# A fused attention layer on one core: the order of GpSimd's work in the last three units, and the first loads cut in halves over two queues

## The chip, the cores and the metric

The kernel runs on one core of a Trainium2 chip. The metric is the time of one execution on the device in microseconds (us), and the time before is the median of three runs. Beside it stands one profiled execution, whose trace gives the start and length of every instruction.

The engines are named as the profile names them: PE (TensorE; PEld is its weight load), DVE (VectorE), ACT (ScalarE), POOL (GpSimd) and SP (SyncE). SP, ACT and POOL also issue DMAs; SPq and ACTq are the issuing side of the first two. SBUF is the on-chip memory, PSUM the accumulators that PE writes.

## The reference, cut to what matters

```python
# x (8, 512, 512); tokens = cond_1024[:, None, :] (8, 1, 512); 16 heads of 32
Q = split_heads(x @ Wq.T + bq);  tQ = split_heads(tokens @ Wq.T + bq)
K = split_heads(x @ Wk.T + bk);  tK = split_heads(tokens @ Wk.T + bk)
V = split_heads(x @ Wv.T + bv)
scores = einsum('bhqd,bhkd->bhqk', Q + tQ, K + tK) / sqrt(32)
out = einsum('bhqk,bhkd->bhqd', softmax(scores), V)
return x + merge_heads(out)
```

All of it is fp32. The projection of the single token (with twice the bias) is a vector per batch and head that is added to Q and K.

## The kernel before, in words

**Units.** A unit t is one batch and one group of four heads, so there are T = 32 units (8 batches by 4 groups). For a unit the kernel computes the scores twice: first with queries on the partitions (`row_scores`, L641), only to take each row's maximum on DVE (L589, L650, L1289) and, for half of the queries, to take the exponentials as well; then with keys on the partitions (L757, L786, L1272), where PE adds the negated row maxima into the same PSUM bank ahead of the scores, so that ACT only has to take exponentials (L767, L796, L1287).

**The split.** To add the maxima on PE exactly enough, a unit's fp32 maxima (128 partitions by 16 numbers) are cut into three bf16 parts: `split_max` (L710 to L719), four small instructions one behind the other, L716 (cast), L717 (subtract), L718 (cast), L719 (subtract). They run on POOL for most units and on DVE for the last two. The parts are then turned so that queries lie along the free dimension: by a DMA transpose (`turn_max`, L728) for most units, by four PE transposes and a copy (`transpose_max`, L738 and L744) for units 0, 30 and 31. The exponentials of a unit can start only behind that.

**Weighted sums.** The exponentials times V (L801, L817), the row sums, the reciprocal (L1049 and others), a 32x32-block transpose on DVE (L889), a multiplication by the reciprocal and the addition of the residual on POOL (`send`, L890 and L891), and four DMAs to the output (L894). The residual is x plus the bias of V: four DMAs (`load_residual`, L191) and one addition on POOL (`bias_residual`, L204), made ahead of `send`.

**Kept exponentials.** For units 1 to 29 (`KEPT`) half of the exponentials of the first pass are kept. They are turned in 32x32 blocks by DVE (L660) and then six pairs of blocks across the diagonal are exchanged by DMA (`swap_kept`, L683) in three moves of six DMAs each: a block aside, its partner into its place, the block from aside to the partner's. Each move waits for the one before. Some of the eighteen are issued by POOL (software queue), the others by SP.

**Order.** The instructions of PE, ACT, DVE and POOL stand in the order in which the program writes them (`manual_schedule`); each engine runs its list strictly in order. SP's list, DMAs alone, is placed by the scheduler. The DMAs of SP and ACT share eight completion counters in turn, so the ninth DMA issued waits until the first has landed, and so on; at the start of the kernel this holds up an issuing queue.

**The start.** Wq's first block of 128 rows is loaded by SP, x's first block by ACT, then x's second by SP and Wk's first by ACT. Then SP loads the three small vectors (`cond`, `bq`, `bk`, L252 to L254), and the rest follows. PE fills the time until data is there with 28 small bf16 matmuls (L933). Then it transposes Wq's block (L313), two blocks of x (L358), Wk's block (L313) and the small vectors (L950), and goes on with projections (L404). ACT loads its function table between its DMAs and its first copy. Wk's remaining columns and Wv follow on SP in strips of 32 rows, 16 DMAs each (L270). `condition` (L911, L913) projects the token by Wq, and later by Wk.

**The end.** Units 29, 30 and 31 have code of their own (from L1294). In unit 30 PE runs three `crossed` rows (`crossed`, L1255 to L1290), each of which computes unit 30's exponentials for a block of keys while DVE takes unit 31's maxima for a block of queries. Behind the third, `split_max(31)` runs on DVE (L1359 of the program writes it), `transpose_max(31)` on PE, and the last unit's four `exponentials` follow, with sums of exponentials on DVE (`sum_of`, L1244 and L1246) and one of them on POOL. In this part POOL also runs: the bias of three residuals, `send` of units 28, 29 and 30, and the sum just named. Unit 31 is finished apart (L1411 to L1438).

Of the kernel before, what the change touches and what calls it, by code (L numbers as in the profile page):

```python
# [17 lines left out]
def kernel(  # L18
# [39 lines left out]
    P = 128  # L58
# [123 lines left out]
    def load_residual(t):  # L182

        b, g = divmod(t, G)
        if turned_by_vector(t):
            if t >= T - 3:
                xr[t] = late[0][:, (t - T + 3) * 4, :].rearrange("p (f e) -> p f e", e=BL)
            else:
                xr[t] = op.tile([P, NB, BL], F32, tag="xr", name=f"xr_{t}")
            for h in range(HG):  # L190
                nc.sync.dma_start(  # L191
                    xr[t][h * BL : (h + 1) * BL], spread(x[b], g * P + h * BL)
                )
        else:

            xr[t] = xT[b][:, g, :]
# [56 lines left out]
    nc.sync.dma_start(cond_sb[B : B + 1, :], bq.rearrange("(o d) -> o d", o=1))  # L253
    nc.sync.dma_start(cond_sb[B + 1 : B + 2, :], bk.rearrange("(o d) -> o d", o=1))  # L254
    load_x(2)
    load_x(3, nc.scalar)
# [6 lines left out]
    nc.scalar.activation(table, ones[:, :1], AF.Exp)  # L263
    load_w("q", Wq, nc.sync, [2, 3])

    for n, w, f in (("k", Wk, HG), ("v", Wv, 0)):
        wn = ws[n].rearrange("p c (f e) -> p c f e", e=BL)
        for cc in range(NC):
            for h in range(HG):
                nc.sync.dma_start(  # L270
                    wn[h * BL : (h + 1) * BL, cc, f:], spread(w, cc * P + h * BL)[:, f:]
                )
    bvl = const.tile([P, 1], F32, tag="bvl", name="bvl")
# [391 lines left out]
    def swap_kept(t, move, last=nc.gpsimd):  # L665
# [6 lines left out]
        for n, (a, g) in enumerate(APART):  # L672
# [10 lines left out]
            (last if here else nc.sync).dma_start(to, of)  # L683
# [248 lines left out]
    for _ in range(28):  # L932
# [27 lines left out]
    transpose_x(3, bank(3), nc.scalar.copy)  # L960
    first_part("k", pk, 0)
# [168 lines left out]
    def thirds(t, made):  # L1130
# [16 lines left out]
        for i in (1, 2):  # L1147
# [29 lines left out]
            if i == 2:  # L1177
                if r == 0:
                    combine_x(b + 1, 1, nc.gpsimd)
                if t + 1 < KEPT[-1]:  # L1180
                    load_residual(t + 1)
# [53 lines left out]

    for t in KEPT[:-1]:
# [57 lines left out]
    late.append(store[:, 4:8].rearrange("p c i s -> p (c i) s"))  # L1294
# [17 lines left out]
    aparts[t] = masked(t)  # L1312
    swap_kept(t, 2)
    halves_of(t - 1, banks(0), (1,))
# [19 lines left out]
    load_residual(t)  # L1334
# [7 lines left out]
    for u in (t, t + 1):  # L1342
        load_residual(u)
    for u in (t + 1, t - 1):
        bias_residual(u)
# [3 lines left out]
    den = denominators_of(t - 1, banks(1))  # L1349
    row(1)  # L1350
# [4 lines left out]
    send_sums(t - 1, whole[t - 1], den)  # L1355
    bias_residual(t)
# [35 lines left out]
    nc.gpsimd.tensor_tensor(y30, y30, rec.broadcast_to([P, NB, BL]), ALU.mult)  # L1392
# [7 lines left out]
    store_30(nc.sync, (0, 1, 3))  # L1400
# [12 lines left out]
    nc.vector.tensor_tensor(part_x[:, two[1]], pd[:, two[1]], xr[t][:, two[1]], ALU.mult)  # L1413
    store_30(nc.scalar, (2,))
    oT = late[0][:, 2, :]
# [56 lines left out]
```

## Time and profile before

| what | value |
|---|---|
| median of 3 runs | 659.02 us (658.79 to 660.39) |
| the profiled execution's own time | 658.57 us |
| its span, first to last instruction | 656.8 us |
| PE busy | 646.9 us (98%) |
| DVE busy | 600.8 us (91%) |
| ACT busy | 534.6 us (81%) |
| POOL busy | 431.1 us (66%) |
| mean granted PE clock | 0.997 |

The span lies 1.77 us below the execution's own time; that part is around the kernel's instructions. A row of the timeline gives the start in us from the start of the span, the length in us, the engine and line, the operation, output and inputs, shapes, the count of instructions that the row merges, and in square brackets how long the engine sat idle before it and what ended that. Neighbouring rows of one engine can overlap by some hundredths, since an instruction's record runs to its last write.

### The profile page before, as it was taken

To read this page: it belongs to the slowest core of one execution; us is meant where nothing else is said; L and a number is where in the kernel's file an instruction comes from. 1 tells how busy PE (TensorE), PEld (TensorE's weight loads), DVE (VectorE), ACT (ScalarE), POOL (GpSimd) and SP (SyncE) were. 2 spreads that over 40 slices of the span, in tenths; PEclk is the share of its full clock that TensorE was granted. 3 is DMA by queue.
4 is the path that set the end of the run, shared out by engine and by line. 5 is a ranking of instruction groups with operands and counts; after the bars stand their busy time and mean duration, and the time that the engine had idled before them with its cause. 6 is when DMAs were issued, how large, how long until landed. Compare 5 with 4: busy or idle time off the path is not lost.

```text
span 656.8 us, 24923 instructions
## 1 busy us (share of the span) xinstructions
PE 646.9 (98%) x9856; PEld 349.5 (53%) x9856; DVE 600.8 (91%) x832; ACT 534.6 (81%) x1364; POOL 431.1 (66%) x680
## 2 busy tenths in 40 slices
PE   9999999999999999999999999999999999999977
PEld 7355455555555555555555555555555555555522
DVE  4799999999999999999999999999999989899897
ACT  2579888889888888988888898888898888887544
POOL 3633665796766777678757667677676776674651
PEclk9999999999999999999999999999999999999989
DMA  7633698988876787877898777787888767687521
GB/s 189 107 49 59 136 182 159 170 175 180 184 158 158 151 186 172 187 156 165 173 194 166 166 164 171 167 180 150 190 190 182 176 146 163 157 148 185 142 46 33
DMA packets 248458, 102.02 MB, mean 155 GB/s; under 512 B 229963, under 2 KB 230475, under 8 KB 248341
## 3 DMA queue, kind: packets, MB, share of 16 engines
q1 hardware_dynamic: 234724, 65.60, 52.6%
q0 software_dynamic: 12384, 33.83, 19.1%
q8 instruction: 78, 1.28, 0.9%
q10 hardware_dynamic: 1232, 0.98, 0.5%
q14 instruction: 40, 0.32, 0.2%
HBM read 19.75 MB, written 8.39 MB: 43 GB/s over the span
## 4 chain that ended last, share of the span: by engine, by line
PE 97%; DVE 1%; DMA 1%; issue 0%; ACT 0%; SPq 0%; DVEq 0%
PE psum L461 44%; PE psum L641 19%; PE psum L817 16%; PE psum L786 8%; PE psum L775 3%; PE psum L404 2%; PE psum L801 2%; PE psum L757 1%; DMA store<-in_x_dram 1%; PE psum L827 0%; PE psum L754 0%; DVE split L718 0%; PE psum L911 0%; PE psum L1272 0%; PE psum L313 0%; PE psum L852 0%
## 5 line engine op out<-in xcount | busy, mean ns | idle before, releaser
L702 ACT ACTIVATE store<-psum,nmax 128x512 f32<-128x512 f32 x204 | 140.1, 701 | 36.0 <-DVE nmax L589 26.3
L702 ACT ACTIVATE psum<-psum,nmax 128x512 f32<-128x512 f32 x248 | 164.7, 669 | 3.6 <-DVE nmax L589 3.0
L683 POOL DMA_DIRECT2D store<-store x258 | 128.7, 502 | 58.4 <-DMA store<-store 40.7
L589 DVE TENSOR_REDUCE nmax<-psum 128x1 f32<-128x512 f32 x225 | 144.4, 678 | 19.0 <-PE psum L641 16.8
L650 DVE TENSOR_REDUCE nmax<-psum 128x2 f32<-128x1024 f32 x125 | 151.4, 1211 | 0.0
L641 PE MATMUL psum<-kT,qT 32*128 32x512 f32 x1024 | 142.5, 617 | 0.0
L796 ACT ACTIVATE store<-psum 128x512 f32<-128x512 f32 x232 | 119.8, 602 | 26.7 <-PE psum L786 26.7
L660 DVE STREAM_TRANSPOSE store<-store 128x1024 f32<-128x1024 f32 x116 | 138.8, 1216 | 0.0
L817 PE MATMUL psum<-store,v 128*32 128x256 f32 x1856 | 106.8, 381 | 0.0
L817 PEld LDWEIGHTS psum<-store,v 128*32 128x32 f32 x1856 | 57.0, 110 | 57.1 <-ACT wT_q L628 21.2
L890 POOL TENSOR_TENSOR res<-res,recs 128x512 f32<-128x512 f32 x30 | 31.4, 1046 | 66.8 <-DVE res L889 66.7
L641 PEld LDWEIGHTS psum<-kT,qT 32*128 32x128 f32 x1024 | 55.7, 183 | 35.5 <-issue 20.0
L786 PE MATMUL psum<-qT,kT 32*128 32x256 f32 x928 | 59.9, 373 | 0.0
L702 ACT ACTIVATION_READ_ACCUMULATOR psum<-psum,nmax 128x1 f32 x248 | 52.7, 213 | 0.0
L461 PE MATMUL psum<-wc_v,xc 128*32 128x256 f32 x768 | 47.7, 379 | 0.0
L786 PEld LDWEIGHTS psum<-qT,kT 32*128 32x128 f32 x928 | 45.5, 184 | 3.9 <-issue 0.3
L204 POOL TENSOR_TENSOR xr<-xr,bvs 128x512 f32<-128x512 f32 x29 | 37.1, 1280 | 11.4 <-DMA x<-in_x_dram 11.4
L461 PE MATMUL psum<-xc,wc_k 128*32 128x256 f32 x720 | 44.5, 379 | 0.0
L461 PE MATMUL psum<-xc,wc_q 128*32 128x256 f32 x720 | 44.5, 379 | 0.0
L702 ACT ACTIVATION_READ_ACCUMULATOR store<-psum,nmax 128x1 f32 x204 | 43.9, 215 | 0.0
L891 POOL TENSOR_TENSOR res<-res,xr 128x512 f32<-128x512 f32 x29 | 37.1, 1278 | 2.3
L461 PE MATMUL psum<-xT,wT_k 128*32 128x256 f32 x480 | 34.5, 382 | 0.0
(196 smaller groups left out, 1001.4 us busy)
## 6 DMA issues: line engine op xcount, KB each, us to landing
store<-store SPq DMA_DIRECT2D x264, 128.0 KB, 2.6
store<-store POOLq DMA_DIRECT2D x258, 128.0 KB, 3.5
out_dram<-res SPq DMA_DIRECT2D x123, 64.0 KB, 3.6
xr<-in_x_dram SPq DMA_DIRECT2D x116, 64.0 KB, 3.0
x<-in_x_dram SPq DMA_DIRECT2D x112, 64.0 KB, 3.4
w_q<-in_L_cond_Wq_dram SPq DMA_DIRECT2D x4, 256.0 KB, 3.9
w_v<-in_L_cond_Wv_dram SPq DMA_DIRECT2D x16, 64.0 KB, 2.4
w_k<-in_L_cond_Wk_dram SPq DMA_DIRECT2D x16, 48.0 KB, 2.6
```

The lines of the kernel that those rows point to most:

```text
L204: nc.gpsimd.tensor_tensor(xr[t], xr[t], bias, ALU.add)
L461: nc.tensor.matmul(pt[r], still[:, r], moving, start=(kc == kcs[0]), stop=(kc == kcs[-1]))
L589: nc.vector.tensor_reduce(nmax[t][:, qc, j : j + 1, 0], pt, AX.X, ALU.max, negate=True)
L641: nc.tensor.matmul(pt, qkT["q", t][r, qc * P : (qc + 1) * P], qkT["k", t][r, :], start=True, stop=True,)
L650: nc.vector.tensor_reduce(nmax[t][:, qc, pr * 2 : pr * 2 + 2, 0], pt, AX.X, ALU.max, negate=True)
L660: nc.vector.transpose(e, e)
L683: (last if here else nc.sync).dma_start(to, of)
L702: nc.scalar.activation(to, of, AF.Exp, bias=nmax[t][:, qc, j, :], accum_out=sums[t][:, qc, j, :],)
L786: nc.tensor.matmul(bank[j][:, i * HS : (i + 1) * HS], qkT["k", t][r, kc * P : (kc + 1) * P], qkT["q", t][r, rest], start=False, stop=(i == 1),
L796: nc.scalar.activation(e[:, i, :], bank[pr * 2 + i], AF.Exp)
L817: nc.tensor.matmul(pt[j * HD : (j + 1) * HD, half * HS : (half + 1) * HS], vs[b % 2][:, kc, (g * HG + j) * HD : (g * HG + j + 1) * HD], e, ...
L891: nc.gpsimd.tensor_tensor(y, y, xr.pop(t), ALU.add)
```

## The change

At the start: Wq's first block and x's first block each come as two halves of 256 columns, the left halves from SP and the right ones from ACT. x's second, third and fourth block and Wk's first are all issued by SP. The small vectors go from SP to ACT, behind the table load. PE's filling matmuls are 24 and not 28. Six of the sixteen strips of Wk are issued by ACT, behind its copy of x's fourth block. `condition("k")` stands right behind `condition("q")`.

At the end: the bias of the residuals of units 29, 30 and 31 and the load of unit 30's stand in unit 29, ahead of the first `crossed` row, and unit 29's residual is loaded in unit 28; both residuals have other places in SBUF (unit 31's is read from the transposed x and needs no load). `send` of unit 29 stands ahead of the second `crossed` row. Unit 30's multiplication by the reciprocal is on DVE, not on POOL. Two of unit 30's four output DMAs go out from ACT and two from SP (before: one and three). The first half of unit 31's last addition stands ahead of the second half of its residual product. In `swap_kept`, unit 28's last move goes wholly to POOL, three DMAs ahead of `split_max(29)` and three behind; unit 29's first move goes wholly to SP.

```diff
-            if t >= T - 3:
-                xr[t] = late[0][:, (t - T + 3) * 4, :].rearrange("p (f e) -> p f e", e=BL)
+            if t == T - 2:
+                xr[t] = late[0][:, 2, :].rearrange("p (f e) -> p f e", e=BL)
...
-    load_w("q", Wq, nc.sync, [0])
-    load_x(0, nc.scalar)
+    xs[0] = early[:, 3, :]
+    for to, of in ((ws["q"][:, 0, :], Wq[:P, :]), (xs[0], x[0, :P, :])):
+        nc.sync.dma_start(to[:, :HS], of[:, :HS])
+        nc.scalar.dma_start(to[:, HS:], of[:, HS:])
     load_x(1)
     wk0 = early[:, 7, :]
-    nc.scalar.dma_start(wk0, Wk[:P, :])
-
-    cond_sb = early[: B + 2, 0, :]
-    nc.sync.dma_start(cond_sb[:B, :], cond)
...
+    nc.sync.dma_start(wk0, Wk[:P, :])
     load_x(2)
-    load_x(3, nc.scalar)
+    load_x(3)
...
     nc.scalar.activation(table, ones[:, :1], AF.Exp)
+    cond_sb = early[: B + 2, 0, :]
+    nc.scalar.dma_start(cond_sb[:B, :], cond)
+    nc.scalar.dma_start(cond_sb[B : B + 1, :], bq.rearrange("(o d) -> o d", o=1))
+    nc.scalar.dma_start(cond_sb[B + 1 : B + 2, :], bk.rearrange("(o d) -> o d", o=1))
...
+    load_spread("k", Wk, HG, (0, 1))
+    load_spread("k", Wk, HG, (2,), nc.sync, (0, 1))
+    load_spread("v", Wv, 0, range(NC))
...
-            if t < KEPT[-2]:
+            if t < KEPT[-1]:
                 here = move == 2 or move == 0 and n >= later
-            elif t < KEPT[-1]:
-                here = move == 2 and n < 3 or move == 0 and n >= later
             else:
-                here = n >= 3
-            (last if here else nc.sync).dma_start(to, of)
+                here = move > 0 and n >= 3
+            (nc.gpsimd if here else nc.sync).dma_start(to, of)
...
-    for _ in range(28):
+    for _ in range(24):
...
     transpose_x(3, bank(3), nc.scalar.copy)
+    load_spread("k", Wk, HG, (2,), nc.scalar, (2, 3))
+    load_spread("k", Wk, HG, (3,), nc.scalar)
...
     condition("q", bank(6))
+    condition("k", bank(5))
     project_qk_part(1, "q", 0, bank(7))
     condition_end("q", bank(1), nc.vector)
     project_qk_end(0, "q", pq)
-    condition("k", bank(5))
...
-                swap_kept(t, 2)
+                first = range(6 if t + 1 < KEPT[-1] else 3)
+                swap_kept(t, 2, first)
                 split_max(t + 1)
                 turn_max(t + 1)
+                swap_kept(t, 2, range(len(first), 6))
...
     swap_kept(t, 1)
     apart = masked(t - 1)
     aparts[t] = masked(t)
+    load_residual(t + 2)
+    bias_residual(t + 2)
     swap_kept(t, 2)
+    bias_residual(t)
+    load_residual(t + 1)
...
     send_sums(t - 1, whole[t - 1], den)
-    load_residual(t)
+    bias_residual(t + 1)
...
     apart = masked(t - 1)
-    for u in (t, t + 1):
-        load_residual(u)
-    for u in (t + 1, t - 1):
-        bias_residual(u)
     halves_of(t - 1, banks(2), (0,))
     nc.scalar.copy(whole[t - 1][:, :HS], banks(2)[:, :HS])
     spread_sums(apart, banks(1))
     den = denominators_of(t - 1, banks(1))
+    send_sums(t - 1, whole[t - 1], den)
     row(1)
     crossed(t, 1, 2)
     acc = room_for_sums(t)
     sum_of(t, acc, 1, nc.gpsimd, [1])
     part_of(t, banks(2), [0])
-    send_sums(t - 1, whole[t - 1], den)
-    bias_residual(t)
     row(2)
...
-    nc.gpsimd.tensor_tensor(y30, y30, rec.broadcast_to([P, NB, BL]), ALU.mult)
+    nc.vector.tensor_tensor(y30, y30, rec.broadcast_to([P, NB, BL]), ALU.mult)
     nc.gpsimd.tensor_tensor(y30, y30, x30, ALU.add)
...
-    store_30(nc.sync, (0, 1, 3))
+    store_30(nc.sync, (0, 1))
...
-    nc.vector.tensor_tensor(part_x[:, two[1]], pd[:, two[1]], xr[t][:, two[1]], ALU.mult)
-    store_30(nc.scalar, (2,))
+    store_30(nc.scalar, (2, 3))
...
         nc.vector.tensor_tensor(oT[:, two[i]], pv[:, two[i]], part_x[:, two[i]], ALU.add)
+        if i == 0:
+            nc.vector.tensor_tensor(part_x[:, two[1]], pd[:, two[1]], xr[t][:, two[1]], ALU.mult)
```

In the first block of the last part, t is unit 29; from "apart = masked(t - 1)" with the two removed loops on, t is unit 30.

More of the change, by code (lines that the diff above doesn't have):

```diff
@@ L663, with swap_kept @@
     between = store[:, 16:18]
-    def swap_kept(t, move, last=nc.gpsimd):
+    def swap_kept(t, move, some=range(6)):
         later = 6 if t % 4 == 1 else 2
@@ L670, in part @@
             return kept[t][a * BL : (a + 1) * BL, g].rearrange("p c h s -> p (c h s)")
-        for n, (a, g) in enumerate(APART):
+        for n in some:
+            a, g = APART[n]
             at = (n + 2) % HG * BL
@@ L1234, in one_item @@
             other_products(n, b, u, dens, nothing, at, True)
+    late.append(store[:, 4:8].rearrange("p c i s -> p (c i) s"))
     for t in KEPT[:-1]:
@@ L1292, in crossed @@
         row_max_of(u, qc, 1, banks(HG + 2, 2))
-    late.append(store[:, 4:8].rearrange("p c i s -> p (c i) s"))
     t = T - 3
@@ L1412 @@
     nc.scalar.copy(den, pd)
-    nc.vector.tensor_tensor(part_x[:, two[1]], pd[:, two[1]], xr[t][:, two[1]], ALU.mult)
-    store_30(nc.scalar, (2,))
-    oT = late[0][:, 2, :]
+    store_30(nc.scalar, (2, 3))
+    oT = late_part(4)
     y = late[0][:, 1, :].rearrange("p (c s) -> p c s", c=NS)
```

13 lines of the change are left out of this document (5 added, 8 removed).

## The prediction

> **What bounds the kernel now.** I read the page first, then PE's waits, then the timeline of the last 50 us and of the first 10.
>
> ```profile
> PE 97%; DVE 1%; DMA 1%; issue 0%; ACT 0%; SPq 0%; DVEq 0%
> ```
>
> This is the chain of work that ended last, by engine: PE carries 97% of it. So an edit pays only where PE waits or behind PE's last work. The waits of PE's matmuls (who waited for whom, us in total, times, longest) name one place:
>
> ```profile
> PE psum L738 <- DVE split L719: 4.0, 1, 4.0
> ...
> PE psum L313 <- DMA w_q<-in_L_cond_Wq_dram: 0.4, 1, 0.4
> ```
>
> Once, for 4.0 us, PE waits for the split of unit 31's maxima; the short waits are at the start. Between, the reader sees PE saturated, by the stretches of the windows view (stretch, its length, then busy time of PE, PEld, DVE, ACT, POOL, granted clock):
>
> ```profile
> 7.00:30.00 23.00, 23.00 (x133) 13.43 (x136) 13.02 (x25) 6.63 (x15) 13.09 (x12) 1.00 0.68 118
> 600.00:630.00 30.00, 30.00 (x408) 14.94 (x404) 25.85 (x39) 18.39 (x40) 11.85 (x20) 1.00 0.63 139
> ```
>
> From 7 us to 30 us and from 600 us to 630 us PE is busy without a gap. Whatever the change moves there costs or gains nothing, unless it creates a wait.
>
> **The split, -3.73 us.** The split of unit 30 (first and last of its four rows), and then unit 31's, beside what POOL does at that time:
>
> ```profile
> 617.16 0.20 DVE L716 CAST split<-nmax 128x16 bf16<-128x16 f32 x1
> 617.92 0.23 DVE L719 TENSOR_TENSOR split<-rest,split 128x16 bf16<-128x16 f32 x1
> ...
> 630.32 0.20 DVE L716 CAST split<-nmax 128x16 bf16<-128x16 f32 x1
> 630.39 1.26 POOL L204 TENSOR_TENSOR store<-store,bvs 128x512 f32<-128x512 f32 x1 [5.74 <-DMA store<-in_x_dram]
> 630.56 1.13 DVE L717 TENSOR_TENSOR rest<-nmax,split 128x16 f32<-128x16 f32 x1
> ...
> 631.62 2.34 POOL L1244 TENSOR_TENSOR acc<-store 128x1024 f32<-128x1024 f32 x1
> 631.73 2.29 DVE L718 CAST split<-rest 128x16 bf16<-128x16 f32 x1
> 633.92 1.04 POOL L890 TENSOR_TENSOR res<-res,recs 128x512 f32<-128x512 f32 x1
> 634.05 0.99 DVE L719 TENSOR_TENSOR split<-rest,split 128x16 bf16<-128x16 f32 x1
> ...
> 635.10 0.40 PE L738 MATMUL psum<-identb,split 128*128 128x128 bf16 x4 [4.00 <-DVE split L719]
> ```
>
> Unit 30's split takes 617.16 to 618.15, 0.99 us. Unit 31's takes 630.32 to 635.04, and each of its slow instructions ends within 0.1 us of the end of the POOL instruction that started just ahead of it: 631.69 against 631.65, 634.02 against 633.96, 635.04 against 634.96. So POOL holds DVE here, an instruction at a time. With POOL idle the split would end at 630.32 + 0.99 = 631.31, and PE would start at 631.37 where it starts at 635.10: 3.73 us.
>
> **Is POOL idle by then?** POOL's late start comes from its first instruction there: it waited 5.74 us for the residual's DMA, which SP issued behind unit 28's output, which waited for POOL.
>
> ```profile
> 622.37 1.29 POOL L891 TENSOR_TENSOR res<-res,xr 128x512 f32<-128x512 f32 x1
> ...
> 623.94 0.18 ACT L1044 COPY den<-psum 128x16 f32<-128x16 f32 x1
> ...
> 624.74 1.29 DVE L1289 TENSOR_REDUCE nmax<-psum 128x1 f32<-128x512 f32 x2 [1.27 <-PE psum L641]
> ...
> 625.68 1.56 SPq L191 DMA_DIRECT2D store<-in_x_dram x3
> 626.71 0.70 PE L641 MATMUL psum<-kT,qT 32*128 32x512 f32 x2
> ...
> 627.23 0.65 DVE L889 STREAM_TRANSPOSE res<-store 128x512 f32<-128x512 f32 x1
> ```
>
> In the changed order unit 30's residual is issued behind unit 29's swap, no longer behind an output, and the biases of units 29 and 31 are added before 621 us, where POOL idles. POOL then runs, by these durations: unit 28's `send` to 623.66 as now; unit 30's bias, 1.26, to 624.9; unit 29's product once DVE has transposed: its reciprocal (0.24 before) can start behind the copy of the denominators, at about 624.2, so the transpose ends at about 625.0; product 1.04 to 626.1; addition 1.27 to 627.4; the sum of exponentials, 2.34, to 629.7. That is 0.6 us ahead of the split at 630.32. The final addition waits for DVE much later.
>
> The moved reciprocal and transpose stand ahead of the second row's maxima, which now begin at 624.74: they begin about 0.3 us later, and PE's next use of those banks, at 626.71, finds them read (625.05 + 1.29 = 626.34). Cost nothing. If POOL's bias held the reciprocal until 624.9, the maxima would begin 0.9 us late and PE would wait some 0.3 to 0.5 us; I keep that as the upper end.
>
> **DVE behind the split, -1.32 us.** From the copy of the turned maxima on DVE works without a gap to the end of the sums, so the end follows DVE:
>
> ```profile
> 635.61 0.42 DVE L744 COPY maxT<-psum 128x512 bf16<-128x512 bf16 x1 [0.56 <-PE psum L738]
> 635.95 1.44 DVE L1244 TENSOR_TENSOR acc<-store 128x1024 f32<-128x1024 f32 x1
> 636.26 2.25 POOL L204 TENSOR_TENSOR store<-store,bvs 128x512 f32<-128x512 f32 x1
> ...
> 637.42 3.31 DVE L1246 TENSOR_TENSOR acc<-acc,store 128x1024 f32<-128x1024 f32 x2
> ...
> 640.66 0.68 DVE L1372 TENSOR_TENSOR parts<-psum,parts 128x512 f32<-128x512 f32 x1
> 641.26 2.34 DVE L1246 TENSOR_TENSOR acc<-acc,store 128x1024 f32<-128x1024 f32 x2
> ...
> 643.52 2.34 DVE L1244 TENSOR_TENSOR acc<-store 128x1024 f32<-128x1024 f32 x2
> ```
>
> An undisturbed pair takes 2.26 us from start to start (641.26 to 643.52). The first sum and the first pair take 637.42 - 635.95 = 1.47 and 640.66 - 637.42 = 3.24 us, because POOL still adds a residual and a bias. Without them: 1.13 and 2.26, so 0.34 + 0.98 = 1.32 us less. PE and ACT kept up with DVE before and start as much earlier as the split ends; if they don't keep up with the faster DVE, up to the 1.32 is lost again. I count it whole, since PE's own slow stretch (below) goes too.
>
> **The tail, -0.5 us.**
>
> ```profile
> 649.77 1.05 POOL L1392 TENSOR_TENSOR res<-res,recs 128x512 f32<-128x512 f32 x1 [11.26 <-DVE res L1390]
> ...
> 650.89 1.26 POOL L1393 TENSOR_TENSOR res<-res,store 128x512 f32<-128x512 f32 x1
> ...
> 652.19 1.41 SPq L1398 DMA_DIRECT2D out_dram<-res  x3
> ...
> 653.71 0.47 SPq L1438 DMA_DIRECT2D out_dram<-store  x1
> ```
>
> The last output, 653.71, waits for SP to issue three others, 0.47 each. The product on DVE costs a quarter of 2.34, 0.59, against 1.12 on POOL (649.77 to 650.89): the addition starts 0.53 us sooner, and SP has two to issue, so it is free 1.0 us sooner. Then unit 31's own data is late instead: its products on DVE stand behind the added 0.59, and half of its last addition is moved forward. I take 0.5, the addition's shift, between 0 and 1.0.
>
> **The start, 0.**
>
> ```profile
> 1.06 3.08 PE L933 MATMUL psum<-onesb 128*128 128x128 bf16 x28 [1.06 <-DVE onesb L259]
> ...
> 4.51 0.63 PE L313 MATMUL psum<-ident,w_q 128*128 128x128 f32 x4 [0.37 <-DMA w_q<-in_L_cond_Wq_dram]
> 6.67 0.39 PE L950 MATMUL psum<-ident,store 10*128 10x10 f32 x4
> ```
>
> And by the table of DMA issues (KB each, us from issue to landing):
>
> ```profile
> bvs<-in_L_cond_bv_dram SPq DMA_DIRECT2D x4, 16.0 KB, 2.1
> ```
>
> Halves on two queues let Wq's block land before x's competes. PE can use that from the end of its shorter filling, 1.06 + 24 x 0.11 = 3.7, and four transposed blocks of 0.63 each bring it to L950 at 6.2 or later. There it needs the small vectors. They leave behind the table load, and by the shared counters the last one waits on ACT until a half of x's block has landed, between 3.7 and 5.1 (the end of the row at 4.51, behind which x's transposes follow). With 2.1 us to landing (that row, for vectors of that kind) that is 5.8 to 7.2, and L950 comes at 6.2 to 7.2 against 6.67 now: a gain of 0.5 to a loss of 0.5. I take 0. ACT's six strips and `condition("k")` change places inside PE's full stretch; I count them at nothing, and at the 0.5 with the rest if a strip is late.
>
> The clock can make the start worse. After PE's 4.0 us of idleness its work was slow:
>
> ```profile
> 628.85 1.06 PE L801 MATMUL psum<-store,v 128*32 128x512 f32 x8
> ...
> 635.43 1.94 PE L801 MATMUL psum<-store,v 128*32 128x512 f32 x8
> ```
>
> The same eight matmuls take 1.94 for 1.06. Four fewer filling matmuls leave PE idle for up to 0.8 us before Wq's block (3.7 to 4.51). Should that slow the clock, the work from 4.51 to 6.67, 2.16 us, would take 1.8 more.
> The Trainium skill, "TensorE: Matmul & The Clock Gate", section "What's actually happening", has PE at half clock until some 3.4 us of sustained work, and so it would count the shorter filling against the change, the 1.8 above; the slow matmuls after the idle agree with its half clock, and no run here shows its threshold.
>
> **The sum.** 3.73 + 1.32 + 0.5 = 5.55 us off the profiled execution's 658.57 gives 653.02. The median of the runs was 0.45 above that execution; I forecast 653.2 for the median.
>
> **Rivals.**
> POOL is still in its sum when the split starts (0.12). The margin is 0.6 us; a later residual or a held reciprocal uses it up. One sum in the way costs up to 2.3: 655.5. Against it: unit 30's residual needs no output first.
> The start loses (0.13): a late small vector, 0.5, or a slow clock, 1.8, beside the end's gain: 653.7 to 655.0.
> It doesn't do what it says (0.04): the split is slow for another reason than POOL, and 658.1 remains, with the tail's 0.5. The matching ends of three pairs speak against it.
> Slower (0.03): unit 29's swap.
>
> ```profile
> 616.53 0.49 POOL L683 DMA_DIRECT2D store<-store  x1 [0.73 <-DMA store<-store]
> ...
> 621.67 1.93 PE L817 MATMUL psum<-store,v 128*32 128x256 f32 x32
> ```
>
> Its last DMA was issued at 616.53, and PE reads the result at 621.67 without waiting. Now a bias of 1.04 us stands ahead of the last three on POOL, and the first move's six on SP alone. Each us beyond 621.67 is a us of PE's; past 5.55 the whole is slower, about 660.5 at 7 us late (659.0 + 7 - 5.5). So it would have to come more than 5.5 us later than now, five times the bias put ahead of it.
>
> **Chances and range.** The forecast itself has 0.68. The measurement can tell about 0.3%, 2 us, from no change. Faster by more: the forecast and the first two rivals, 0.93; within: the third, 0.04; slower: 0.03. The range goes from 651.8 (653.02 less the start's 0.5 and 0.5 more in the tail, and a little below) to 655.6 (POOL in the way); 656 and more is left out.
>
> **What would show it.** Right: unit 31's split in about 1.0 us, ending at about 631.3 on the old clock of the trace; no POOL row between 630 and 636; PE's wait for L719 gone or under 0.5; DVE's pairs all near 2.3; the last SP issue right behind DVE's last product. Wrong: a POOL row across the split, a wait of PE at L950 or in the swap's reader, or a gap on DVE among the sums.

## The result, and the profile after

The changed kernel takes 656.59 us (median of 13 runs, 654.83 to 659.91) against 660.12 us of before beside it (658.57 to 663.01): ratio 0.9948, with a 95% interval of 0.9929 to 0.9967, so 3.4 us less (2.2 to 4.7). The forecast was 653.2 for a median of 659.02, a ratio of 0.9912. The direction was right; 0.0036, or 2.4 us, of the expected gain is missing, and the time lies above the range. Part of the distance to 653.2 is that before was itself 1.1 us slower in this measurement than the 659.02 that the forecast started from: as a ratio, the range's upper end (655.6 of 659.02) is 0.9948.

The profiled execution was the slowest of the changed kernel's 13, 659.91 us with a span of 658.0, while that of before was the fastest of its own. So spans are not compared here, but stretches of the two traces. First the waits of PE's matmuls on the changed kernel's page (who waited for whom, us in total, times, longest):

```profile
PE psum L779 <- DMA maxT<-split: 1.7, 1, 1.7
PE psum L954 <- DMA store<-in_L_cond_bq_dram: 1.6, 1, 1.6
PE psum L742 <- DVE split L723: 1.2, 2, 1.0
```

The 4.0 us for unit 31's split are gone. Three waits stand there that before did not have: at the small vectors (L954 is before's L950), at a turn of maxima in the middle (L779, before's L775), and 1.0 us at a split, unit 30's now. The end of the changed kernel's timeline (the split's lines are L720 to L723, before's L716 to L719):

```profile
633.66 2.37 POOL L1252 TENSOR_TENSOR acc<-store 128x1024 f32<-128x1024 f32 x1
...
636.51 0.20 DVE L720 CAST split<-nmax 128x16 bf16<-128x16 f32 x1
...
637.20 0.23 DVE L723 TENSOR_TENSOR split<-rest,split 128x16 bf16<-128x16 f32 x1
...
637.49 0.40 PE L742 MATMUL psum<-identb,split 128*128 128x128 bf16 x4 [0.20 <-DVE split L723]
637.99 0.42 DVE L748 COPY maxT<-psum 128x512 bf16<-128x512 bf16 x1 [0.56 <-PE psum L742]
...
649.27 0.71 DVE L1391 STREAM_TRANSPOSE store<-psum 128x512 f32<-128x512 f32 x1
...
654.59 0.41 SPq L1445 DMA_DIRECT2D out_dram<-store  x1
```

And from before, beside the rows that the prediction shows:

```profile
648.07 0.70 DVE L1385 STREAM_TRANSPOSE store<-psum 128x512 f32<-128x512 f32 x1
```

POOL's sum ends at 636.03, 0.48 us ahead of the split, and the split takes 0.92 us. From its first cast to the copy of the turned maxima it is 1.48 us, where before had 630.32 to 635.61, 5.29: **3.81 less**. From the copy to DVE's transpose of the denominators it is 11.28 where before had 12.46 (635.61 to 648.07): **1.18 less**. From there to the last issue of an output it is 5.32, before 5.64: **0.32 less**. So the end gives 5.31 us in this trace.

The start gives much of it back. The changed kernel, then before:

```profile
3.59 1.06 PE L318 MATMUL psum<-ident,w_q 128*128 128x128 f32 x4
...
4.41 0.23 ACTq L264 DMA_DIRECT2D store<-in_L_cond_bk_dram  x1
...
8.62 0.38 PE L954 MATMUL psum<-ident,store 10*128 10x10 f32 x4 [1.63 <-DMA store<-in_L_cond_bq_dram]
8.94 2.98 PE L409 MATMUL psum<-xT,wT_q 128*128 128x256 f32 x8
...
11.71 1.78 PE L363 MATMUL psum<-ident,store 128*128 128x128 f32 x8
...
13.32 1.89 PE L409 MATMUL psum<-xT,wT_k 128*128 128x256 f32 x8
```

```profile
6.99 1.99 PE L404 MATMUL psum<-xT,wT_q 128*128 128x256 f32 x8
8.82 1.04 PE L358 MATMUL psum<-ident,store 128*128 128x128 f32 x8
9.69 1.89 PE L404 MATMUL psum<-xT,wT_k 128*128 128x256 f32 x8
```

bq is issued at 3.59 and bk at 4.41, each when a half block loaded by ACT has landed and freed its counter (at 3.57 and 4.39). The profile names bq as what PE waited for, but by the landing times in the trace bq was there at 7.68 and bk at 8.53, 0.09 us ahead of PE's matmul: PE was held by bk, which took 4.1 us to land. PE waits 1.63 us, and behind the wait the same work takes 2.98 for 1.99 and 1.78 for 1.04, at a granted clock of 0.50 from 9.80 to 13.20. The projection of K stands at 13.32 for 9.69, and every matmul with turned maxima from 45 us to 500 us stands 3.4 us later than in before: nothing in the full stretch pays it back. Some 0.5 us of this is a good draw of before's: in fill_split and end_only (below), which keep before's start, the projection of K stands at 10.20 and 10.32.

Unit 30's split:

```profile
622.19 1.28 POOL L204 TENSOR_TENSOR xr<-xr,bvs 128x512 f32<-128x512 f32 x1
...
622.33 1.22 DVE L720 CAST split<-nmax 128x16 bf16<-128x16 f32 x1
...
624.39 0.40 PE L742 MATMUL psum<-identb,split 128*128 128x128 bf16 x4 [0.97 <-DVE split L723]
```

In before this cast took 0.20 and PE did not wait. Now the bias of unit 29's residual, 1.28 us on POOL, lies across it, and the cast ends with it.

### The profile page after: what moved, and what is told of

The parts are those of the page before. It is cut to its first block, busy times and chain, and to the rows that moved or that the text cites. A ratio compares the mean times of both kernels' runs of the same rounds, so it can differ in the third digit from the quotient of the medians.

```text
span 658.0 us, 24910 instructions
## 1 busy us (share of the span) xinstructions
PE 647.9 (98%) x9852; PEld 351.0 (53%) x9852; DVE 597.6 (91%) x833; ACT 534.3 (81%) x1364; POOL 429.1 (65%) x679
## 3 DMA queue, kind: packets, MB, share of 16 engines
q8 instruction: 78, 1.28, 0.8%
```

## The experiments

The theory: the end does what was forecast, and the missing time is lost at the start, by the small vectors, and in unit 30's split. Rivals: the end gains less than it seems; the slow clock at the start comes from the shorter filling; the first profile is an accident. Times are medians in us, each beside runs of before on the same chip.

| kernel | median | before | ratio (95% interval) |
|---|---|---|---|
| changed | 656.59 | 660.12 | 0.9948 (0.9929 to 0.9967) |
| start_only | 661.00 | 659.82 | 1.0019 (1.0003 to 1.0036) |
| end_only | 654.96 | 659.82 | 0.9921 (0.9905 to 0.9938) |
| vec_sp | 655.27 | 659.82 | 0.9925 (0.9909 to 0.9941) |
| fill16 | 656.35 | 659.82 | 0.9944 (0.9926 to 0.9963) |
| after_again | 656.39 | 659.87 | 0.9953 (0.9937 to 0.9968) |
| vec_bias | 654.71 | 659.87 | 0.9924 (0.9907 to 0.9941) |
| fill_split | 659.18 | 659.87 | 0.9990 (0.9980 to 0.9999) |
| start8 | 653.55 | 659.87 | 0.9906 (0.9892 to 0.9920) |
| after_bias | 655.86 | 659.41 | 0.9951 (0.9935 to 0.9968) |
| sum_twice | 655.78 | 659.41 | 0.9954 (0.9942 to 0.9966) |
| tail_pool | 653.56 | 659.41 | 0.9914 (0.9901 to 0.9926) |
| vec_late | 659.95 | 659.60 | 1.0005 (0.9996 to 1.0014) |

### start_only: the start by itself

Before with the hunks of the diff from the first loads to `condition("k")`:

```diff
+    for to, of in ((ws["q"][:, 0, :], Wq[:P, :]), (xs[0], x[0, :P, :])):
...
+    nc.scalar.dma_start(cond_sb[:B, :], cond)
...
-    for _ in range(28):
+    for _ in range(24):
```

> Before's program with the start of the changed one alone (halves on two queues, small vectors on ScalarE's queue, 24 filling matmuls, six strips on ScalarE, both conditions together); everything from unit 1 on is before's. Theory (the start loses, because the small vectors come late): PE waits about 1.6 us for bq ahead of the transposes of the small vectors (L950 of before at about 8.6 instead of 6.67), the projection behind them runs at half clock (about 3.0 us for 2.0), and from there on every row stands 3.4 us later; time 3.4 us above before, near 663.5. Rival (the profiled execution of the changed kernel was an odd one, and the start costs little in most runs): no wait at that place and a time within 1 us of before.

Measured: 1.2 us above before (0.2 to 2.4), so the start by itself loses, but a third of what the theory gave. Nine of the twelve runs lie between 659.66 and 661.66, three between 663.58 and 664.42. Its timeline:

```profile
6.07 0.67 PE L363 MATMUL psum<-ident,store 128*128 128x128 f32 x4 [0.57 <-DMA store<-in_x_dram]
...
7.63 0.38 PE L955 MATMUL psum<-ident,store 10*128 10x10 f32 x4 [0.18 <-issue]
```

With the same order of issues bk, issued at 4.37, landed at 7.54 here, and PE had spent 0.57 us waiting for x's second block instead. So the 3.4 us of the first profile were a bad draw: three of the twelve runs lie about that far up (3.8 to 4.6 us above before's median), though no trace shows what held them up. The theory's number does not hold; of the rival, the missing wait holds in this trace (0.18 us), and a time within 1 us of before is not shown.

### end_only: the end by itself

Before with the diff's other hunks:

```diff
-    for u in (t, t + 1):
-        load_residual(u)
-    for u in (t + 1, t - 1):
-        bias_residual(u)
...
+    send_sums(t - 1, whole[t - 1], den)
     row(1)
...
-    nc.gpsimd.tensor_tensor(y30, y30, rec.broadcast_to([P, NB, BL]), ALU.mult)
+    nc.vector.tensor_tensor(y30, y30, rec.broadcast_to([P, NB, BL]), ALU.mult)
```

> Before's start with the end of the changed program alone (order of GpSimd's work, the swap's queues, the product on VectorE, the stores). Theory: unit 31's split takes 1.0 us, the sums behind it run at 2.3 us a pair, the tail is 0.3 us shorter, together -5.3 us; unit 30's split is hit by a bias on GpSimd, +1.0 us; so 4.3 us below before, near 655.8, and below the changed kernel by what the start loses. Rival (the end gains less than the trace seems to show, since a DMA turn of the maxima comes late in the middle because of the swap's new queues): a wait of 1 to 2 us of PE for a turn is there again near 500 us, and the time is 2.5 us below before.

Measured: ratio 0.9921, 5.2 us less (4.1 to 6.3). With start_only's +0.0019 that makes 0.9940, which the changed kernel's interval holds. Its end:

```profile
617.08 1.28 POOL L204 TENSOR_TENSOR xr<-xr,bvs 128x512 f32<-128x512 f32 x1
...
617.78 0.65 DVE L715 CAST split<-nmax 128x16 bf16<-128x16 f32 x1
...
619.28 0.40 PE L737 MATMUL psum<-identb,split 128*128 128x128 bf16 x4 [0.40 <-DVE split L718]
...
632.88 0.42 DVE L743 COPY maxT<-psum 128x512 bf16<-128x512 bf16 x1 [0.56 <-ACT store L766]
...
644.16 0.71 DVE L1384 STREAM_TRANSPOSE store<-psum 128x512 f32<-128x512 f32 x1
...
649.49 0.41 SPq L1438 DMA_DIRECT2D out_dram<-store  x1
```

Copy to transpose is 11.28 and transpose to last issue 5.33, as in the changed kernel's first trace. The bias meets the split again, for 0.4 us of PE this time. There is no wait for a turn of maxima near 500 us.

### vec_sp, fill16, after_again: what the vectors cost

vec_sp and fill16 are the changed kernel with one edit each, vec_sp's first; after_again is the changed kernel itself.

```diff
     nc.sync.dma_start(wk0, Wk[:P, :])
+    nc.sync.dma_start(cond_sb[:B, :], cond)
+    nc.sync.dma_start(cond_sb[B : B + 1, :], bq.rearrange("(o d) -> o d", o=1))
+    nc.sync.dma_start(cond_sb[B + 1 : B + 2, :], bk.rearrange("(o d) -> o d", o=1))
     load_x(2)
...
-    nc.scalar.dma_start(cond_sb[:B, :], cond)
```

```diff
+    for _ in range(16):
+        nc.tensor.matmul(pc[:, :P], onesb, onesb, start=True, stop=True)
     for cc in range(NC):
         nc.tensor.transpose(
```

> The changed kernel with one edit: the three small vectors go out from SP, right behind Wk's first block and ahead of x's third. Theory (the late small vectors are the start's loss, by the wait and by the half clock that follows the idle): PE does not wait at L954's transposes, which come at about 7.0; the projection behind them takes 2.0 us and not 3.0; time 3.0 us below the changed kernel, near 653.5. Rival (only the wait goes, and the clock is slow for another reason, the shorter filling): the projection still takes about 3.0 us and the time is 1.6 us below the changed kernel. Second rival (Wq's and x's later blocks, now behind the vectors, are late instead): a new wait of PE behind the projection and no gain.

> The changed kernel with 16 more small matmuls on PE directly ahead of the small vectors' transposes, so that PE is busy while it waits for them (16 x 0.11 = 1.8 us). Theory (the idle slows the clock): the transposes still come at about 8.7, but the projection behind them takes 2.0 us (3.0 in the changed kernel) and x's third and fourth block 1.05 (1.78): 1.7 us below the changed kernel. Rival (the clock is slow anyway): both stay as slow, and the time is the changed kernel's or 0.2 more.

> The changed kernel once more, as the measure for the others of this call. Theory (bq's landing at the start and the landing of a turn of the maxima are matters of luck, which fell badly in the first profile): the wait ahead of the small vectors' transposes is below 1.0 us this time, no wait for a turn near 500 us, time 3.5 us below before (656.5). Rival (the start loses 3.4 us every time): the wait of 1.6 us and the half clock behind it are there again.

vec_sp came to 0.9925, against 0.9948 and 0.9953 of the changed kernel's two measurements: 1.5 to 1.8 us less, not 3.0. The timeline of vec_sp, then of fill16, then of after_again:

```profile
7.20 0.41 PE L954 MATMUL psum<-ident,store 10*128 10x10 f32 x4
7.54 1.99 PE L409 MATMUL psum<-xT,wT_q 128*128 128x256 f32 x8
```

```profile
7.11 1.06 PE L954 MATMUL psum<-onesb 128*128 128x128 bf16 x16
8.10 0.41 PE L956 MATMUL psum<-ident,store 10*128 10x10 f32 x4
8.44 1.99 PE L409 MATMUL psum<-xT,wT_q 128*128 128x256 f32 x8
```

```profile
7.47 0.38 PE L954 MATMUL psum<-ident,store 10*128 10x10 f32 x4
7.79 1.99 PE L409 MATMUL psum<-xT,wT_q 128*128 128x256 f32 x8
```

Where PE does not sit idle at this place, the projection takes 1.99 us, with the same 24 filling matmuls: so the shorter filling is not what slowed it, and the rival to vec_sp falls; the second too, since no wait follows behind the projection. fill16 keeps the clock fast but always spends 1.06 us, and its median is not told apart from the changed kernel's; its 1.7 us were wrong. after_again's profiled execution took 654.17 us, with a wait of 0.11 us at the vectors, none near 500 us and none in unit 30's split. But the median is 656.39 again, and the runs go to 658.35.

The vectors set this place in every trace of the changed start in which PE was free: bk lands at 8.53 (changed), 7.54 (start_only), 7.45 (after_bias) and 7.38 (after_again), and each time PE begins their transposes 0.09 us later, with waits of 1.63, 0.18, 0.69 and 0.11 us. With the vectors on SP bk is there by 6.15 and 6.22 (vec_sp, vec_bias). So their landing differs from execution to execution; that this alone spreads the runs is not shown, since only profiled executions have a trace.

### vec_late: the same cost, made larger

On vec_bias (below), whose vectors are early:

```diff
-    nc.sync.dma_start(cond_sb[B : B + 1, :], bq.rearrange("(o d) -> o d", o=1))
-    nc.sync.dma_start(cond_sb[B + 1 : B + 2, :], bk.rearrange("(o d) -> o d", o=1))
...
     load_w("q", Wq, nc.sync, [2, 3])
+    nc.sync.dma_start(cond_sb[B : B + 1, :], bq.rearrange("(o d) -> o d", o=1))
+    nc.sync.dma_start(cond_sb[B + 1 : B + 2, :], bk.rearrange("(o d) -> o d", o=1))
```

> The kernel with the vectors on SP and the bias ahead of the swap, with bq and bk moved on SP behind Wq's four blocks, later than in any other kernel here. They would be issued at about 5.6 to 6.1 (3.0 and 3.6 without the move), and with 3 to 4 us to landing the small vectors' transposes come at 9.0 to 10.0 instead of 6.6. Theory (the small vectors' lateness is what the changed start loses, by the wait itself and by the slow clock that follows an idle of more than about 1.5 us): PE waits 2.0 to 3.0 us there, the projection behind takes about 3.0 us and not 2.0, every row of the middle stands about 4 us later, and the time is about 4 us above the kernel with early vectors: ratio to before 0.9985. Rival (the changed kernel's typical loss has another source, and the wait in its first profile was an accident without weight): the wait is there, but PE regains it later, and the ratio stays at 0.9925 to 0.995.

```profile
6.79 0.24 SPq L265 DMA_DIRECT2D store<-in_L_cond_bk_dram  x1
...
7.05 1.06 PE L318 MATMUL psum<-ident,store 128*128 128x128 f32 x4
...
11.24 0.57 PE L954 MATMUL psum<-ident,store 10*128 10x10 f32 x4 [3.13 <-DMA store<-in_L_cond_bq_dram]
11.74 3.78 PE L409 MATMUL psum<-xT,wT_q 128*128 128x256 f32 x8
```

Measured: 1.0005, 5.3 us above vec_bias (0.0081 of 659.6; about 4 was expected). bk, issued at 6.79 behind Wq's blocks, lands at 11.15, 4.4 us later; PE waits 3.1 us; the projection takes 3.78. But PE was slow ahead of this wait already: Wk's block takes 1.06 at 7.05, where after_again's takes 0.66. So the 3.78 can't be put down to the wait alone, and in this trace the price of the wait and that of a clock that was slow from the start are mixed. The matmuls with turned maxima stand 7.0 us later than in before from 45 us to 616 us. Issuing two vectors of 2 KB later undoes the whole gain of the end. The rival (PE regains it) falls.

### vec_bias, after_bias: the bias in unit 30's split

The same edit on vec_sp and on the changed kernel:

```diff
+    bias_residual(t)
     swap_kept(t, 2)
-    bias_residual(t)
     load_residual(t + 1)
```

> The kernel with the small vectors on SP, and unit 29's bias on GpSimd put ahead of the last move of unit 29's swap instead of behind it, so that GpSimd is idle when unit 30's maxima are split. Theory (GpSimd's bias holds VectorE's first cast): that cast takes 0.20 us (1.22 in the changed kernel), PE's wait there falls from 1.0 to 0.2 or less, and the time is 0.9 us below the kernel with the vectors alone: 5.5 us below before, ratio 0.9915. Rival (PE waits there for the maxima themselves, or for the swap, whose last three DMAs now stand behind the bias): the cast is short, but a wait of about 1 us comes at the swap's reader, and the time stays.

> The changed kernel with one edit: unit 29's bias ahead of the last move of unit 29's swap. The small vectors stay on ScalarE's queue. Theory (two things keep the changed kernel from its forecast, the late small vectors and the bias in unit 30's split, and this takes away the second alone): the first cast of unit 30's split takes 0.20 us, ratio to before 0.9940, between the changed kernel's 0.995 and the 0.9924 of the kernel with both edits. Rival (the bias costs little in the median, since it is hit in some runs only): ratio 0.995 as the changed kernel's. Second rival (the bias was all of it): 0.9924 or below.

In the trace it does what was expected. after_bias:

```profile
616.98 1.26 POOL L204 TENSOR_TENSOR xr<-xr,bvs 128x512 f32<-128x512 f32 x1
...
619.14 0.20 DVE L720 CAST split<-nmax 128x16 bf16<-128x16 f32 x1
```

In the medians it does not show: 0.9951 against 0.9953 for the changed kernel, 0.9924 against 0.9925 for vec_sp. The traces say that it should cost something: of the five kernels with the bias in its first place, four were hit, and PE lost 1.05 (vec_sp), 0.97 (changed), 0.89 (fill16) and 0.40 us (end_only); only in after_again did the bias end at 617.71 and the cast begin at 617.70. By the two intervals each pair of medians tells only differences over some 1.5 us (an estimate), so what the bias costs on average, up to about 1 us, stays open. The two pairs with late and early vectors agree: 0.9953 to 0.9925 and 0.9951 to 0.9924, **1.8 us for moving the vectors** either way, with an interval of some 0.7 to 2.9 us for both pairs together (estimated from the four intervals).

after_bias's trace has a wait for a turn of maxima near 500 us, as the changed kernel's first one:

```profile
501.54 0.40 PE L779 MATMUL psum<-maxT,onesb 3*128 3x512 bf16 x4 [1.29 <-DMA maxT<-split]
```

Of the traces of all kernels here, only these two have it; after_again and fill16, whose vectors are on ACT's queue too, do not.

### sum_twice: does POOL hold the split?

On start8 (below):

```diff
-    sum_of(t, acc, 1, nc.gpsimd, [1])
+    for _ in range(2):
+        sum_of(t, acc, 1, nc.gpsimd, [1])
```

> The kernel with eight first transfers and the bias ahead of the swap, in which GpSimd forms its sum of exponentials twice, one right behind the other (the same operands into the same place). The second sum, 2.37 us, stands across the split of unit 31 (630.9 to 633.2, where the split would take 631.38 to 632.30). Theory (GpSimd holds VectorE an instruction at a time): one of the split's four instructions ends within 0.1 us of the end of the second sum, the split takes about 2.6 us instead of 0.92, PE waits about 1.9 us instead of 0.20, and the time is 1.5 to 2.0 us above the kernel without it (653.6): 655.3. Rival (the split was slow in before for another reason than GpSimd's large operations): the split stays near 0.92 us and the time within 0.3.

```profile
626.93 4.79 POOL L1251 TENSOR_TENSOR acc<-store 128x1024 f32<-128x1024 f32 x2
...
629.79 2.00 DVE L719 CAST split<-nmax 128x16 bf16<-128x16 f32 x1
...
632.56 0.61 PE L741 MATMUL psum<-identb,split 128*128 128x128 bf16 x4 [2.00 <-DVE split L722]
633.10 1.94 PE L804 MATMUL psum<-store,v 128*32 128x512 f32 x8
```

The second sum ends at 631.72; the cast, 128 by 16 numbers that take 0.20 us by themselves, ends at 631.79; PE waits 2.00 us. The time is 2.2 us above tail_pool on the same chip, and 3.2 us above start8 by the ratios, more than the expected 1.5 to 2.0; PE's slow clock behind the wait (1.94 for 1.06) would explain the surplus, which no run tests apart. So POOL holds DVE until its instruction ends. It does not hold all that DVE does: in the changed kernel's trace DVE's reductions from PSUM beside POOL's sum (at 634.05 and 635.26) take 1.29 for two and 1.22 us, as elsewhere. The Trainium skill, "SBUF — State Buffer", section "SBUF: two separate sides", calls the pair of ports that DVE and GpSimd share an exclusive lock, held for the whole instruction, and lets only some of DVE's operations need it: those in a two-port mode and those with two inputs from SBUF. The 2.00 us agree with its length; that the cast, which has one input, runs in that mode no run here shows.

### fill_split: the clock behind the 4 us

On before:

```diff
+    for _ in range(56):
+        nc.tensor.matmul(bank(5)[:, :P], onesb, onesb, start=True, stop=True)
     transpose_max(t + 1, bank(5), nc.vector.tensor_copy)
```

> The kernel before, with 56 small matmuls on PE (about 3.7 us) ahead of unit 31's transposes of the maxima, so that PE is busy while GpSimd holds VectorE; the hold itself stays. Theory (the idle makes PE's clock slow behind it, for a time that differs from run to run, and this is why before spreads from 659.1 to 663.0): the eight matmuls behind the split take 1.06 us and not 1.94, the spread falls below 1.5 us, and the median falls by 1.0 us. Rival (VectorE's sums bound the end, so PE's clock there does not matter): the matmuls are fast again and the time stays within 0.5 us.

```profile
635.67 0.40 PE L738 MATMUL psum<-identb,split 128*128 128x128 bf16 x4 [0.86 <-DVE split L719]
636.00 1.06 PE L801 MATMUL psum<-store,v 128*32 128x512 f32 x8
```

The matmuls take 1.06 instead of 1.94, the runs lie within 1.5 us (658.70 to 660.18) where before's beside them span 3.4 (658.60 to 661.96), and the median falls by 0.7 (0.1 to 1.3). That lies between theory (1.0) and rival (under 0.5), and the interval holds both; some 0.7 us of before's median go with the slow clock. The spread shows less than it seems: the eleven runs of before beside after_bias span 1.5 us too (658.52 to 660.02), with nothing filled, so that the slow clock makes before's spread is not shown. The rest of what the end gains falls to the hold of the split and of the sums by subtraction.

### start8 and tail_pool: a faster version, and its tail

start8 is the changed kernel with vec_bias's edit at the bias and the start of the first diff; tail_pool is start8 with the second, which puts the product back on GpSimd.

```diff
+    nc.sync.dma_start(ws["q"][:, 0, :HS], Wq[:P, :HS])
+    nc.scalar.dma_start(ws["q"][:, 0, HS:], Wq[:P, HS:])
+    load_x(0)
+    load_x(1, nc.scalar)
...
     nc.sync.dma_start(wk0, Wk[:P, :])
+    nc.sync.dma_start(cond_sb[:B, :], cond)
```

```diff
-    nc.vector.tensor_tensor(y30, y30, rec.broadcast_to([P, NB, BL]), ALU.mult)
+    nc.gpsimd.tensor_tensor(y30, y30, rec.broadcast_to([P, NB, BL]), ALU.mult)
```

> As the kernel with the vectors on SP and the bias ahead of the swap, and the start again with eight transfers that need no counter of another: Wq's first block in two halves from SP and ScalarE, x's first block whole from SP, x's second from ScalarE, Wk's first and the small vectors from SP. Theory (in the changed start the ninth transfer waits for a counter, and x's second block comes late as the fifth transfer): no wait of PE for x's second block (0.5 us in the kernels with four halves), the small vectors' transposes at 6.7 or earlier, 0.5 us below the kernel with four halves. Rival (the sum of the bytes sets when x's second block is there): the same wait, the same time.

> The same kernel (eight first transfers, bias ahead of the swap) with unit 30's product by the reciprocal back on GpSimd; the stores stay two and two. Theory (the product on VectorE shortens the path to unit 30's output, but unit 31's own products stand behind it there): the last issue of an output comes 0.3 us later than with the product on VectorE, against its copy of the turned maxima; in the time this is 0.05% and can't be told apart. Rival (the last output follows unit 31's products on VectorE, which come earlier without the added one): the last issue comes 0.3 us or more earlier.

start8 is the fastest kernel of all, 0.9906 (0.9892 to 0.9920), with runs from 653.33 to 654.44; tail_pool has the same median. That beats the changed kernel by 2.8 to 3.1 us (0.9906 against 0.9948 and 0.9953). The 0.5 us expected against four halves can't be told from vec_bias's 0.9924. In start8's trace the vectors' transposes came at 7.12, not 6.7, behind a wait of 0.18 us for x's first block; tail_pool and sum_twice, which have the same start, have them at 6.38 and 6.25, and none of the three waits for x's second block.

start8's trace also has a wait that no other has:

```profile
618.07 0.49 POOL L686 DMA_DIRECT2D store<-store  x1 [0.25 <-issue]
...
622.72 1.93 PE L820 MATMUL psum<-store,v 128*32 128x256 f32 x32 [0.72 <-ACT store L1294]
```

These matmuls read unit 29's swapped blocks. The profile names ACT, but the first of ACT's pieces was done at 621.70, and in before PE began 0.24 us behind that piece. The swap's last transfer, issued at 618.07 with the bias now ahead of it (616.53 in before), took 4.5 us and landed at 622.53. So the rival of vec_bias's expectation, a wait at the swap's reader, did come here, for 0.72 us; in vec_bias itself the last transfer landed at 620.83, 0.69 us before PE read it.

The tail, start8's timeline and then tail_pool's:

```profile
632.86 0.42 DVE L747 COPY maxT<-psum 128x512 bf16<-128x512 bf16 x1 [0.56 <-ACT store L770]
...
649.45 0.41 SPq L1444 DMA_DIRECT2D out_dram<-store  x1
```

```profile
631.30 0.42 DVE L747 COPY maxT<-psum 128x512 bf16<-128x512 bf16 x1 [0.56 <-ACT store L770]
...
647.02 0.76 DVE L1438 TENSOR_TENSOR store<-psum,rec 128x256 f32<-128x256 f32 x2
...
647.84 0.41 SPq L1444 DMA_DIRECT2D out_dram<-store  x1
```

Copy to last issue is 16.59 with the product on DVE and 16.54 with it on POOL: no difference, so both expectations fail. The last output goes out right behind DVE's last product (647.02 + 0.76 = 647.78), whichever engine did unit 30's.

## Why the prediction was right and where it failed

**The split, -3.73: right.** 3.81 in the trace, POOL idle 0.48 us ahead of it (0.6 forecast), and sum_twice shows the hold on purpose. The rival "POOL is still in its sum" did not come.

**The moved reciprocal and transpose, 0: right.** From unit 30's turn on PE to the first cast of unit 31's split it is 12.12 us in both traces (624.39 to 636.51; 618.20 to 630.32).

**DVE behind the split, -1.32: right, a little large.** 1.18. The first sum takes 1.25 from start to start (638.33 to 639.58), not 1.13; the first pair 2.28, as forecast.

**The tail, -0.5: mis-sized, by a wrong path.** 0.32. The prediction let unit 30's addition set the end; tail_pool shows that it does not. In before DVE's last product ended at 653.36 (652.61 + 0.75), and SP issued at 653.71, behind its third output: 0.35 us of waiting for SP, which is what went.

**The start, 0: the step that failed.** The measured loss is 1.2 us for the whole start (start_only, 0.2 to 2.4) and 1.8 for moving the vectors (two pairs); whether the rest of the start gains the difference, the intervals don't tell. The term that was mis-sized is the vectors' landing. That the last one leaves between 3.7 and 5.1 was right: bk left at 3.92 to 4.41 in the four traces of this start (changed, start_only, after_again, after_bias). But 2.1 us was the median of vectors loaded later in a quieter queue; with blocks of 256 KB issued ahead of it, bk took 3.2 to 4.1 us, and PE's transposes came at 7.47 to 8.62, each time beyond the forecast's 6.2 to 7.2. Before's own trace had this price: there bk, issued at 2.38, landed at 6.53, 4.2 us later and just ahead of L950 at 6.67, and no wait showed it because PE was busy until then. With 4.2 for 2.1 the prediction's own sum gives 7.9 to 9.3.

The rival put the late vector at 0.5 *or* the slow clock at 1.8; in the first trace the wait brought the slow clock with it. The four fewer filling matmuls, which the rival blamed, left no idle: Wq's halves were there at 3.59, before the filling ended. PE's earlier beginning did not pay in full, though: the first block's transposes took 1.06 us at 3.59, where before's trace has 0.63 at 4.51 (and 1.09 at 4.28 in end_only, with all 28 filling matmuls). And the sum had no term for x's second block, for which PE waits 0.46 to 0.57 us in five of the traces with four halves.

**A contention not seen.** The prediction had the biases of units 29 and 31 added "before 621 us, where POOL idles". Unit 30's split stands at 617.16 in the rows quoted there. Taking off the 5.18 us by which L779 is late from 500 us on in the changed kernel's trace (504.72 for 499.54 in before), the bias came at 617.0, into the split. It is the same mechanism that the change was read to remove, one unit earlier; PE lost between 0 and 1.05 us to it in five traces.

**The swap, the slower rival: did not come in the changed kernel.** None of its traces has PE waiting for unit 29's swap; start8's, with unit 29's bias ahead of the last move as well, has 0.72 us.

**The account.** Missing were 2.4 us: 1.8 from the vectors, 0.24 from the end's sum (5.55 against 5.31), and what is left lies within the measurements' intervals and the open cost of the bias. This account fits, but it is not measured term by term: the 1.8 has an interval of some 0.7 to 2.9, and the waits for a turn of maxima (1.67 us in one of the changed kernel's two traces, 1.29 us in after_bias's) have no term in it. The forecast also wrote 653.2 where its own sum, 653.02 and 0.45, makes 653.5. With the vectors early, the bias ahead of the swap and eight transfers, the ratio is 0.9906, where the forecast had 0.9912; since that start is another than the one forecast, the agreement is in part luck.

## What to carry to other kernels

A small load that the first stage needs must be priced by what is ahead of it when it is issued, not by the median landing of its kind; here the trace of before held that price, hidden because PE was busy. In a saturated kernel each us at the start is paid in full, and with interest when the idle slows PE. When work is moved off one critical stretch of an engine, look through all stretches of the same kind, above all the one that the moved work now stands beside. Take several profiles before a wait of one trace is made a term of the sum.

## What the runs showed of the hardware

**Idle and clock.** PE was slow (1.94 for 1.06, or 2.98 for 1.99), at a granted clock of 0.50, behind idles of 1.63 (changed), 2.00 (sum_twice), 4.00 (before) and 4.18 us (start_only); the slow stretch lasted 3.4 us in the changed kernel and in before, and 6.8 us in the other two. It was not slow behind 0.86 (fill_split), 0.97 and 1.05 (unit 30's split in the changed kernel and vec_sp) and 1.29 us (after_bias). vec_late's 3.13 us tell nothing, as PE was slow before them. And behind 1.67 us in the middle of the changed kernel,

```profile
498.06 1.23 SPq L732 DMA_TRANSPOSE maxT<-split  x1
...
504.72 0.40 PE L779 MATMUL psum<-maxT,onesb 3*128 3x512 bf16 x4 [1.67 <-DMA maxT<-split]
```

nothing was lost beyond the wait: the granted clock is 1.00 from 504 to 508, and L779 was 3.4 us late before it and 5.2 behind it. So the "about 1.5 us" of vec_late's expectation is no threshold. The Trainium skill, "TensorE: Matmul & The Clock Gate", section "What's actually happening", has the clock fall after an idle window of about 3.4 us whose phase is free; 1.63 and 2.00 us were enough here, so a whole such window of idle was not needed, while the slow stretches of 3.4 and 6.8 us agree with the window's length, and its free phase would fit the unequal outcomes. No run here tests the phase.

**A drifting DMA queue.** In the fence above, the turn of the maxima is issued 6.7 us ahead of the matmul that it holds up. In end_only this lead is 9 us or more for every unit; in several traces it shrinks in the middle of the kernel, to 5.5 us in before, and recovers behind 500 us. In the two traces with a wait it had shrunk from about 140 us on. vec_late, whose vectors are the latest, keeps 8.3 us or more, which speaks against late vectors as the cause; what it is stays open.
